# A state-space network on one core: the late plan with decays in SBUF, one slice summed on TensorE, and projections of two chunks at a time

## The chip, the cores and the metric

The program runs on one NeuronCore of a Trainium2 chip. The metric is the device time of one execution in microseconds; each kernel is given by the median of several runs. TensorE is called PE, VectorE DVE, ScalarE ACT, GpSimd POOL, and SyncE, which issues the transfers, SP.

## The reference

The network has two layers over a 64 x 64 image with 96 channels. Each layer is a mixer and then a small MLP on the 4096 tokens, both with a residual. The mixer of the second layer is what matters here. It normalizes, projects to 192 inner channels and a gate, convolves, and then scans the image in four directions, with 16 states for each channel:

```python
dA = jnp.exp(dt_t[..., None] * A)
h = dA * h + (dt_t * u_t)[..., None] * B_t[:, None, :]
y = jnp.sum(h * C_t[:, None, :], axis=-1)
...
yy = y[0] + wh_y + inv_y[0] + invwh_y
yy = yy * jax.nn.silu(z)
return yy @ W_out.T
```

The MLP normalizes each token over its 96 channels, rounds to an 8-bit float, multiplies to 384 hidden units, adds a bias, takes the relu, rounds again and multiplies back to 96:

```python
h = jax.nn.relu(_qlinear(x, W1, b1))
y = _qlinear(h, W2, b2)
```

## The kernel before

The scans of the second layer are tiled by six groups of 32 channels and four quarters of the 16 states. A tile has 128 partitions, 32 channels times 4 states, and 4096 positions in time, in four slices of 1024. So there are 24 passes, one for each group and quarter. A pass scans rows and columns, forward and backward: 16 scan instructions of 1024 elements on DVE (`scan`, line 2007). A scan needs two inputs. One is the decay, an exponential that ACT computes in `decay_into` (line 1992); it lies in `two`, two PSUM tiles of 1024 columns named `da`, which the scans use in turn. The other is the input product in SBUF, which POOL makes. After the scans of a slice POOL adds the two column scans into `hs` (`add_columns`, line 2012), PE adds the row scans to it with identity matrices (lines 2018 and 2022), ACT fetches the sum, POOL multiplies it by C (`times_c`, line 2035), and PE folds the four states of a channel into the accumulator `acc` (`sum_states`, line 2046). After four passes a group is complete.

For most of the passes the order of this work is written out by hand, by positions in the sequence of scans. The end is different. From the position `first_late` on, in the middle of the last pass, instructions are collected in an object of the class `Order`. Each has an engine, a price, what it reads, writes and takes from a pool of buffers, and an urgency `lead`, set for each chunk from the list `LATE`. `Order.run` then lists them on their engines by the prices. Only the order in which each engine is given its instructions comes out of this, and the waits follow from the data. An engine takes its instructions strictly in that order.

The late plan holds the last ten scans, the products of the last pass, the gate, the output projection, and the MLP of all tokens, in eight chunks of 512 tokens. Its steps, in the order of the data:

- The projection of channel group four for chunks 4 to 7 (`early`, lines 2312 and 2314): PE puts the residual chunk and the product of `ye`, the stored result of that group, into a bank, and ACT copies the sum back to `res` (line 2323). For other groups and chunks this has been done in the passes before.
- For slices `a` in `BY_SUMS`, PE adds the row scans and `hs` in a bank (line 2332), ACT fetches that (2346), and POOL multiplies by C (2348). For other slices POOL adds (2352) and multiplies (2353).
- The last row scans `x2s` are multiplied by C by DVE or POOL in halves of 512 (line 2358; POOL for the slices in `TIMES_POOL`). PE folds both products into `acc` (2282). Line 2285 adds the skip term.
- DVE multiplies `acc` by the gate (2363). PE projects, for each of the two chunks in a slice, with 32 rows and 96 columns at a time (`mixed`, 2371), and DVE adds the bank to `res` (2392).
- MLP (`late_chunk`): DVE takes statistics (2397), ACT and DVE make the inverse root (2400, 2401), DVE normalizes by token column in four pieces of 96 (2405), PE transposes (2411), ACT copies (2414), PE multiplies by the first weights (2418), ACT or DVE casts from PSUM (2420, `ROUND_DVE`), DVE or ACT adds the bias and takes the relu (2424 and 2422, `RELU_ACT`), POOL casts to 8 bits (2425), PE multiplies by the second weights (2430), ACT copies (2433), DVE or POOL adds the bias (2435, `BIAS_POOL`) and the residual (2437, `LAST_POOL`), and SP stores the chunk (2438).

The late plan keeps its buffers in free parts of `x0s` and `x1s`, and takes PSUM banks from `late` and, once the last scan has read its decay, from `da`.

Of the kernel before, what the change touches and what calls it, by code (L numbers as in the profile page):

```python
# [126 lines left out]
BY_SUMS, TIMES_POOL = (0, 1), (0, 3)  # L127
ROUND_DVE, RELU_ACT = [(2, 2), (5, 1), (5, 2), (6, 2), (7, 0)], [(0, 1), (2, 1), (5, 0), (7, 1)]
BIAS_POOL, LAST_POOL = (0, 1, 6), (0, 1, 2, 3)
LATE = (103.0, 38.0, -4.0, -6.0, -9.0, -12.0, -12.0, -13.0)  # L130
# [125 lines left out]
class Net:  # L256
# [1636 lines left out]
    def scans(self, xs, out):  # L1893
# [14 lines left out]
        with ExitStack() as ctx:  # L1908
# [208 lines left out]
            def load_y(f, m):  # L2117
                rows = (slice(0, P), slice(P, P + GC))[f]
                if f == 0 or m == 0:
                    self.ye = self.ye[::-1]  # L2120
                to = slice(GC * (m % 3), GC * (m % 3) + GC) if f else slice(0, P)
                inputs[f, m] = self.ye[0][to], self.tail_w[f][to]
                keep(nc.sync.dma_start(self.ye[0][to], self.y_d[rows, chunk(m)]))
# [15 lines left out]
            pairs += [(1, i, k) for i, k in ((n - 3, 2), (n - 2, 2), (n - 1, 3)) for k in range(k)]  # L2139
# [95 lines left out]
            for p in range(first_late + 1, len(seq)):  # L2235
                i, o, e = seq[p]
                das[p] = das[pos[i, o, e - 1]] if e == NS else 1 - das[p - 1]
# [22 lines left out]
            own, ident8, b2h = carve(P), carve(P, FP8, 1), carve(CD, F16, 2)  # L2260
            for tag, k, form in (
                ("st", 4, lambda: carve(12).rearrange("p (j s) -> p j s", s=3)),
                ("sd", 4, lambda: carve(4)),
                ("x8", 3, lambda: tokens(carve(4 * CD, FP8, 1))),
                ("xt", 3, lambda: carve(CH, BF16, 2)[0:CD]),
                ("h16", 6, lambda: carve(CH, F16, 2)),
                ("h8", 3, lambda: carve(nm * CH, FP8, 1).rearrange("p (m t) -> p m t", m=nm)),
                ("o16", 3, lambda: tokens(carve(4 * CD, F16, 2))),
            ):
                od.slots(tag, [form() for _ in range(k)])  # L2270
            od.slots("bank", [ph.tile([P, CH], F32, tag="hs", name=f"late{i}") for i in range(2)])
            od.slots("hc", [hcs[(NS * last + a) % 3] for a in range(2)])
# [4 lines left out]
            od.add("POOL", 0.3, lambda: keep(pool.tensor_copy(b2h, b2)), w=["b2h"])  # L2277

# [10 lines left out]
            od.add("SEQ", 0.0, lambda: od.free["hc"].append((0.0, hcs[(NS * last + 2) % 3])), r=["times", "sums"], w=["third"])  # L2289
# [9 lines left out]
            def open_banks():  # L2299
                od.free["bank"] += [(0.0, t[:, h * CH : (h + 1) * CH]) for t in two for h in range(nh)]  # L2300

            od.add("SEQ", 0.0, open_banks, r=[("S", 0, both - 1), ("da", 0), ("da", 1)], w=["open"])
# [5 lines left out]
            def early(m):  # L2308
                def f():
                    y, w = inputs.pop((1, m))  # L2310
                    o = tokens(at["eo", m][:, 0 : 4 * CD])
                    keep(nc.tensor.matmul(o, self.ident, self.res[:, m], start=True, stop=False))
                    for j in range(4):
                        keep(nc.tensor.matmul(o[:, j], y[:, j:CH:4], w, start=False, stop=j == 3))

                return f

            for m in range(4, NCH):
                if m == 7:
                    od.add("SP", 0.65, lambda: load_y(1, 7), w=[("ye", 1)], kb=64)  # L2320
                od.lead = LATE[m]
                od.add("PE", 1.6, early(m), r=[("ye", m % 3)], new={("eo", m): "bank"})
                od.add("ACT", 0.46, lambda m=m: keep(act.copy(self.res[:, m], tokens(at["eo", m][:, 0 : 4 * CD]))), r=[("eo", m)], w=[("res", m)])

# [3 lines left out]
            def presum(a, h):  # L2328
                def f():
                    s = chunk(turn[last % 2][1][a] * nh + h)  # L2330
                    for k, t in enumerate((h0, hs)):
                        keep(nc.tensor.matmul(at["s", a, h], self.ident, t[:, s], start=k == 0, stop=k == 1))  # L2332
# [3 lines left out]
            for a in range(NS):  # L2336
# [5 lines left out]
                A = ("A", a)  # L2342
                if a in BY_SUMS:
                    for h in range(nh):
                        od.add("PE", 1.8, presum(a, h), r=ready, new={("s", a, h): "bank", **({("hc", a): "hc"} if h == 0 else {})})
                        od.add("ACT", 0.6, lambda a=a, h=h: keep(act.copy(at["hc", a][:, half(h)], at["s", a, h])), r=[("s", a, h), ("hc", a)], w=[(A, h)])
                    for h in range(nh):
                        od.add("POOL", 1.27, lambda a=a, h=h, t=times: keep(pool.tensor_tensor(at["hc", a][:, half(h)], at["hc", a][:, half(h)], t[:, half(h)], ALU.mult)), r=[("hc", a)], w=[(A, h)])
                    od.add("PE", 0.95, lambda a=a, m0=m0: fold([at["hc", a][:, half(h)] for h in range(nh)], m0, False), r=[("hc", a), (A, 0), (A, 1)], w=[A])
                else:  # L2350
                    t = hs[:, part[j]]
                    od.add("POOL", 2.36, lambda t=t, j=j: keep(pool.tensor_tensor(t, t, h0[:, part[j]], ALU.add)), r=ready, w=[(A, 0)])
                    od.add("POOL", 2.36, lambda t=t, c=times: keep(pool.tensor_tensor(t, t, c, ALU.mult)), r=[(A, 0)], w=[(A, 0)])
                    od.add("PE", 0.95, lambda t=t, m0=m0: fold([t[:, half(h)] for h in range(nh)], m0, False), r=[(A, 0)], w=[A])
                xp = x[:, part[j]]
                for h in range(nh):
                    e, cost = ((nc.vector, 0.67), (nc.gpsimd, 1.27))[a in TIMES_POOL]
                    od.add(("DVE", "POOL")[a in TIMES_POOL], cost, lambda e=e, h=h, xp=xp, t=times: keep(e.tensor_tensor(xp[:, half(h)], xp[:, half(h)], t[:, half(h)], ALU.mult)), r=[("S", 0, NS + a)], w=[("xc", a, h)])
                od.add("PE", 0.95, lambda xp=xp, m0=m0: fold([xp[:, half(h)] for h in range(nh)], m0, True), r=[A, "sums", ("skip", m0 // NQ), ("xc", a, 0), ("xc", a, 1)], w=[("fx", a)])

                b, q = divmod(m0, NQ)
                r = slice(GC * q, GC * q + nh * GC)
                od.add("DVE", 0.72, lambda r=r, b=b: keep(dve.tensor_tensor(gu[r, b], acc[r, b], gz[r, b], ALU.mult)), r=[("fx", a)], w=[("y", a)])

                def mixed(m0=m0):
                    for j in range(4):
                        for m in range(m0, m0 + nh):
                            b, q = divmod(m, NQ)
                            r = slice(GC * q, GC * q + GC)
                            o = tokens(at["o", m][:, 0 : 4 * CD])  # L2370
                            keep(nc.tensor.matmul(o[:, j], gu[r, b, j:CH:4], self.tail_w[2][r], start=True, stop=True))

                od.add("PE", 1.1, mixed, r=[("y", a)], new={("o", m): "bank" for m in range(m0, m0 + nh)})
# [5 lines left out]
    def late_chunk(self, od, m, ov, ident8, b2h):  # L2379
# [7 lines left out]
        st, sd, x8, xt, h8, o16 = ((k, m) for k in ("st", "sd", "x8", "xt", "h8", "o16"))  # L2387
# [3 lines left out]

        od.add("DVE", 0.58, lambda: keep(dve.tensor_tensor(x, x, tokens(at["o", m]), ALU.add)), r=[("o", m)], w=[("res", m)])
# [6 lines left out]
        od.add("DVE", 0.56, stats, r=[("res", m)], new={st: "st"})  # L2399
        od.add("ACT", 0.3, lambda: keep(act.activation(at[sd], at[st][:, :, 2], AF.Sqrt, bias=self.eps5, scale=1.0 / CD)), r=[st], new={sd: "sd"}, table="sqrt")  # L2400
        od.add("DVE", 0.17, lambda: keep(dve.reciprocal(at[sd], at[sd])), w=[sd])

        def normed():
            for j in range(4):
                keep(dve.tensor_scalar(at[x8][:, j], x[:, j], at[st][:, j, 1:2], at[sd][:, j : j + 1], ALU.subtract, ALU.mult, saturate=False))

        od.add("DVE", 0.68, normed, r=[("res", m), st, sd], new={x8: "x8"})
# [5 lines left out]
        od.add("PE", 0.55, turned, r=[x8, "ident8"], new={("t", m): "bank"})  # L2413
        od.add("ACT", 0.6, lambda: keep(act.copy(at[xt], at["t", m][0:CD])), r=[("t", m)], new={xt: "xt"})
        for i in range(nm):
# [3 lines left out]
            e, f, cost = (("ACT", act.copy, 0.6), ("DVE", dve.tensor_copy, 0.65))[(m, i) in ROUND_DVE]  # L2419
            od.add(e, cost, lambda f=f, h=h, k=k: keep(f(at[k], at[h])), r=[h], new={k: "h16"})  # L2420
            if (m, i) in RELU_ACT:
                od.add("ACT", 0.65, lambda k=k, b=b: keep(act.activation(at[k], at[k], AF.Relu, bias=b)), w=[k])
            else:
                od.add("DVE", 0.42, lambda k=k, b=b: keep(dve.tensor_scalar(at[k], at[k], b, 0.0, ALU.add, ALU.max)), w=[k])
# [7 lines left out]
        od.add("PE", 1.0, down, r=[h8, *(("h8", m, i) for i in range(nm))], new={("f", m): "bank"})  # L2432
        od.add("ACT", 0.47, lambda: keep(act.copy(at[o16], tokens(at["f", m]))), r=[("f", m)], new={o16: "o16"})
        e, f, cost = (("DVE", dve, 0.3), ("POOL", pool, 0.8))[m in BIAS_POOL]
        od.add(e, cost, lambda f=f: keep(f.tensor_tensor(at[o16], at[o16], b2h.unsqueeze(1).to_broadcast([P, 4, CD]), ALU.add)), r=["b2h"], w=[o16])
        e, f, cost = (("DVE", dve, 0.58), ("POOL", pool, 0.9))[m in LAST_POOL]
        od.add(e, cost, lambda f=f: keep(f.tensor_tensor(x, x, at[o16], ALU.add)), r=[o16], w=[("res", m)])
        od.add("SP", 0.65, lambda: keep(nc.sync.dma_start(ov[:, m], x)), r=[("res", m)], kb=192)
# [126 lines left out]
```

## Time and profile before

| What | Value |
|---|---|
| Runs | 1263.56 us median of 3, 1262.83 to 1267.61 |
| Profiled execution | 1267.05 us, of which the span is 1265.2 us |
| PE, matmuls | 1042.1 us busy, 82% of the span |
| DVE | 1138.5 us busy, 90% |
| ACT | 884.0 us busy, 70% |
| POOL | 847.7 us busy, 67% |
| Start of the first late scan | 1177.74 us |
| Last store issued | 1262.2 us |

Busy time is the time in which an engine has an instruction of the program in work, also if that instruction stands and waits for something inside the engine. The span begins with the first instruction and ends with the last one; the rest of the execution's time lies around it. A group of instructions is shown with its line in the kernel, the engine, the operation, output and inputs by the program's names, shapes, count, busy time and mean duration in nanoseconds, and then the idle time of the engine just before these instructions with what ended it.

### The profile page before, as it was taken

To read this page: it belongs to the slowest core of one execution; us is meant where nothing else is said; L and a number is where in the kernel's file an instruction comes from. 1 tells how busy PE (TensorE), PEld (TensorE's weight loads), DVE (VectorE), ACT (ScalarE), POOL (GpSimd) and SP (SyncE) were. 2 spreads that over 40 slices of the span, in tenths; PEclk is the share of its full clock that TensorE was granted. 3 is DMA by queue.
4 is the path that set the end of the run, shared out by engine and by line. 5 is a ranking of instruction groups with operands and counts; after the bars stand their busy time and mean duration, and the time that the engine had idled before them with its cause. 6 is when DMAs were issued, how large, how long until landed. Compare 5 with 4: busy or idle time off the path is not lost.

```text
span 1265.2 us, 11505 instructions
## 1 busy us (share of the span) xinstructions
PE 1042.1 (82%) x3666; PEld 427.2 (34%) x3666; DVE 1138.5 (90%) x922; ACT 884.0 (70%) x1068; POOL 847.7 (67%) x517
## 2 busy tenths in 40 slices
PE   9998988987367788897778877787778889898886
PEld 7632233322122222332222222333223444333434
DVE  6395698577989999999999999999999999999787
ACT  4455566545677878888778877888778878777435
POOL 3000385243277878978888878988888878976566
PEclk9999989997578888888878889898789999888875
DMA  2062110146755665545735675545736766423201
GB/s 74 13 171 77 26 26 13 50 152 209 232 172 158 224 219 196 149 137 178 243 126 157 224 209 206 148 139 175 239 126 196 241 210 222 149 80 93 78 1 51
DMA packets 79134, 183.17 MB, mean 145 GB/s; under 512 B 21534, under 2 KB 34936, under 8 KB 77688
## 3 DMA queue, kind: packets, MB, share of 16 engines
q1 hardware_dynamic: 78376, 182.16, 45.7%
q8 instruction: 31, 0.51, 0.2%
q14 instruction: 39, 0.32, 0.1%
q10 hardware_dynamic: 688, 0.19, 0.1%
HBM read 159.73 MB, written 21.52 MB: 143 GB/s over the span
## 4 chain that ended last, share of the span: by engine, by line
DVE 41%; PE 15%; issue 9%; ACT 4%; DMA 2%; POOL 1%; SPq 0%; another core or an unknown queue 0%; POOLq 0%; DVEq 0%; ACTq 0%
DVE xws L2007 13%; DVE h1s L2007 12%; DVE h0s L2007 7%; PE hs L2018 6%; PE hs L2022 3%; DVE x1s L2007 3%; DVE x0s L2007 2%; DVE x2s L2007 2%; ACT da L1992 2%; ACT xws L1977 1%; DMA kept<-xn 1%; PE acc L2046 1%; POOL hss L2012 1%; DMA x2s<-bc 1%; PE late L2332 1%
## 5 line engine op out<-in xcount | busy, mean ns | idle before, releaser
L2035 POOL TENSOR_TENSOR kept<-kept,kept 128x1024 f32<-128x1024 f32 x92 | 216.9, 2358 | 81.9 <-issue 39.8
L2012 POOL TENSOR_TENSOR hss<-h1s,xws 128x1024 f32<-128x1024 f32 x96 | 228.1, 2378 | 60.0 <-DVE xws L2007 57.2
L2018 PE MATMUL hs<-h0s,ident 128*128 128x512 f32 x360 | 220.1, 697 | 28.0 <-DVE h0s L2007 24.1
L1992 ACT ACTIVATE da<-dt1s,a 128x1024 f32<-128x1024 f32 x168 | 187.5, 1117 | 69.3 <-DVE xws L2007 54.7
L2007 DVE TENSOR_TENSOR_SCAN xws<-da,xws 128x1024 f32<-128x1024 f32 x96 | 222.1, 2313 | 12.4 <-ACT da L1992 12.3
L1992 ACT ACTIVATE da<-dt0s,a 128x1024 f32<-128x1024 f32 x166 | 185.1, 1116 | 39.7 <-DVE h0s L2007 16.1
L2022 PE MATMUL hs<-hss,ident 128*128 128x512 f32 x368 | 189.1, 606 | 21.4 <-POOL hss L2012 21.4
L2007 DVE TENSOR_TENSOR_SCAN h1s<-da,h1s,xws 128x1024 f32<-128x1024 f32 x72 | 167.6, 2328 | 0.8 <-ACT da L1992 0.5
L2046 PE MATMUL acc<-kept,fold 128*32 128x512 f32 x368 | 88.7, 694 | 68.5 <-POOL kept L2035 68.5
L2031 ACT COPY kept<-hs 128x512 f32<-128x512 f32 x184 | 107.1, 582 | 48.5 <-PE hs L2022 47.7
L2018 PEld LDWEIGHTS hs<-h0s,ident 128*128 128x128 f32 x360 | 71.3, 215 | 152.8 <-issue 82.3
L2022 PEld LDWEIGHTS hs<-hss,ident 128*128 128x128 f32 x368 | 69.4, 193 | 120.6 <-issue 78.8
L2018 PE MATMUL hs<-x0s,ident 128*128 128x512 f32 x128 | 73.5, 658 | 13.8 <-DVE x0s L2007 13.8
L2018 PE MATMUL hs<-x1s,ident 128*128 128x512 f32 x128 | 72.4, 650 | 13.4 <-DVE x1s L2007 13.4
L1971 POOL TENSOR_TENSOR x1s<-x1s,dus 128x1024 f32<-128x1024 f32 x32 | 75.5, 2361 | 8.8 <-DMA x1s<-bc 8.8
L2018 PE MATMUL hs<-x2s,ident 128*128 128x512 f32 x120 | 67.5, 646 | 14.5 <-DVE x2s L2007 14.5
L1971 POOL TENSOR_TENSOR x2s<-x2s,dus 128x1024 f32<-128x1024 f32 x32 | 75.8, 2367 | 0.3 <-DMA x2s<-bc 0.3
L2007 DVE TENSOR_TENSOR_SCAN x0s<-da,x0s 128x1024 f32<-128x1024 f32 x32 | 74.0, 2313 | 1.1 <-ACT da L1992 1.1
L2007 DVE TENSOR_TENSOR_SCAN x1s<-da,x1s 128x1024 f32<-128x1024 f32 x32 | 74.0, 2313 | 1.1 <-ACT da L1992 1.1
L2007 DVE TENSOR_TENSOR_SCAN x2s<-da,x2s 128x1024 f32<-128x1024 f32 x32 | 74.1, 2316 | 0.9 <-ACT da L1992 0.7
L1244 POOL MEMSET pairs<- 96x256 f32 x1 | 0.3, 308 | 103.3 <-ACTq L309 103.3
L1977 ACT COPY xws<-x1s 128x1024 f32<-128x1024 f32 x32 | 63.4, 1980 | 5.2 <-POOL hss L2012 5.2
(372 smaller groups left out, 1973.7 us busy)
## 6 DMA issues: line engine op xcount, KB each, us to landing
kept<-bc SPq DMA_DIRECT2D x92, 512.0 KB
x2s<-bc SPq DMA_DIRECT2D x32, 512.0 KB
x0s<-bc SPq DMA_DIRECT2D x28, 512.0 KB
x1s<-bc SPq DMA_DIRECT2D x28, 512.0 KB
dus<-du SPq DMA_DIRECT2D x20, 512.0 KB
dt1s<-dt SPq DMA_DIRECT2D x20, 512.0 KB
dt0s<-dt SPq DMA_DIRECT2D x20, 512.0 KB
kept<-xn SPq DMA_DIRECT2D x24, 384.0 KB
```

The source lines that it names most:

```text
L1244: nc.gpsimd.memset(self.pairs1[:, :, 0 : HW + 2 : HW + 1, :], 0.0)
L1971: keep(nc.gpsimd.tensor_tensor(x, x, du[:, part[j]], ALU.mult))
L1977: keep(copy(grid(xw)[:, w, :], cols(xs[i % 3])[:, w, :]))
L1992: keep(nc.scalar.activation(t, dts[o][:, part[j]], AF.Exp, scale=self.a6[:, g, k : k + 1]))
L2007: keep(nc.vector.tensor_tensor_scan(to, da, x, start, ALU.mult, ALU.add))
L2012: keep(nc.gpsimd.tensor_tensor(cols(hs)[:, w, :], grid(h1)[:, w, :], grid(xw)[:, w, :], ALU.add))
L2018: keep(nc.tensor.matmul(t, self.ident, x[:, chunk(m)], start=k == 0, stop=False))
L2022: keep(nc.tensor.matmul(sums[i, m], self.ident, hs[:, chunk(m)], start=False, stop=True))
L2031: keep(nc.scalar.copy(to, sums.pop((i, j * (SC // CH) + h))))
L2035: keep(nc.gpsimd.tensor_tensor(t, t, times_c_by(i, a), ALU.mult))
L2046: keep(nc.tensor.matmul(to, self.fold4, src, start=k == 0, stop=k == NK - 1))
L2332: keep(nc.tensor.matmul(at["s", a, h], self.ident, t[:, s], start=k == 0, stop=k == 1))
```

## The change

The late plan is given new settings and new steps.

- Nine of the ten late scans read their decay from two new SBUF tiles, carved from `x0s`. The PSUM tiles `da` serve as banks as soon as the first late scan is done.
- Only slice 0 is summed on PE, now with the last row scans `x` too. DVE multiplies this sum by C from the bank, and ACT's fetch and POOL's product of it are gone. Slices 1 to 3 are added and multiplied on POOL. The products of the last row scans of slices 1 and 3 go to POOL, those of slice 2 to DVE.
- The projection works on two chunks at once. Two tiles `blocks` hold the weights of a group twice, on the diagonal of a 64-row block, so one matmul takes 64 rows in and gives 192 columns. For chunks 4 to 7 the product of group four opens the banks in which the product of the last group is then added. The residual is no longer put through PE, and DVE adds each bank to half of two chunks of `res`. The load of `ye` for chunk 7 is issued with those of chunks 4 to 6.
- The normalization is two operations of 384 elements with broadcast statistics on DVE (five chunks) or four pieces on ACT (three chunks).
- Relus, casts, bias and last adds are shared out anew: relus go to POOL in nine cases, to ACT in six and to DVE in nine; one bias add and no last add is left on POOL.
- Prices and urgencies are new.

```diff
-BY_SUMS, TIMES_POOL = (0, 1), (0, 3)
-ROUND_DVE, RELU_ACT = [(2, 2), (5, 1), (5, 2), (6, 2), (7, 0)], [(0, 1), (2, 1), (5, 0), (7, 1)]
-BIAS_POOL, LAST_POOL = (0, 1, 6), (0, 1, 2, 3)
-LATE = (103.0, 38.0, -4.0, -6.0, -9.0, -12.0, -12.0, -13.0)
+BY_SUMS, TIMES_POOL = (0,), (1, 3)
+ROUND_DVE = ((1, 1), (1, 2), (2, 0), (3, 0), (4, 2), (5, 1), (7, 0))
+RELU_ACT = ((1, 0), (3, 0), (3, 2), (5, 0), (6, 0), (7, 0))
+RELU_POOL = ((0, 0), (0, 1), (1, 1), (1, 2), (2, 0), (2, 1), (2, 2), (3, 1), (4, 0))
+NORM_ACT, BIAS_POOL, LAST_POOL = (1, 3, 4), (0,), ()
+LATE = (266.0, 520.0, 182.0, 420.0, -46.0, -128.0, -287.0, 1415.0)
...
-                das[p] = das[pos[i, o, e - 1]] if e == NS else 1 - das[p - 1]
+                das[p] = das[pos[i, o, e - 1]] if e == NS else 5 - das[p - 1] if p > first_late + 1 else 2
...
+            blocks = [carve(2 * CD) for _ in range(2)]
+            two += [carve(SC) for _ in range(2)]
...
-            od.add("SEQ", 0.0, open_banks, r=[("S", 0, both - 1), ("da", 0), ("da", 1)], w=["open"])
+            od.add("SEQ", 0.0, open_banks, r=[("S", 1, NS)], w=["open"])
...
+            def blocked(key, y, w, r, first, end):
                 def f():
+                    for k in range(2):
+                        o = at[key, k][:, 0 : 4 * CD].rearrange("p (j e) -> p j e", j=2)
+                        for j in range(2):
+                            keep(nc.tensor.matmul(o[:, j], y[r, 2 * k + j : CH : 4], w[r], start=first and j == 0, stop=end and j == 1))
...
+                        od.add("PE", 0.9, summed(a, h, h0, True, False), r=ready[-1:], new={key: "bank"})
+                        od.add("PE", 0.9, summed(a, h, hs, False, False), r=whole, w=[key])
+                        od.add("PE", 0.9, summed(a, h, x, False, True), r=[("S", 0, NS + a)], w=[key])
+                        od.add("DVE", 0.69, lambda h=h, xp=xp, t=times, key=key: keep(dve.tensor_tensor(xp[:, half(h)], at[key], t[:, half(h)], ALU.mult)), r=[key], w=[("xc", a, h)])
...
+        if m in NORM_ACT:
+            od.add("DVE", 0.18, rate, r=[sd], w=[st])
+            od.add("ACT", 1.2, normed, r=[*both, st, sd], new={x8: "x8"})
+        else:
+            od.add("DVE", 0.6, lambda: keep(dve.tensor_tensor(at[xc], x, spread(at[st][:, :, 1]), ALU.subtract)), r=[*both, st], new={xc: "xd"})
+            od.add("DVE", 0.57, lambda: keep(dve.tensor_tensor(at[x8], at[xc], spread(at[sd]), ALU.mult, saturate=False)), r=[xc, sd], new={x8: "x8"})
...
             if (m, i) in RELU_ACT:
-                od.add("ACT", 0.65, lambda k=k, b=b: keep(act.activation(at[k], at[k], AF.Relu, bias=b)), w=[k])
+                od.add("ACT", 0.74, lambda k=k, b=b: keep(act.activation(at[k], at[k], AF.Relu, bias=b)), w=[k])
             else:
-                od.add("DVE", 0.42, lambda k=k, b=b: keep(dve.tensor_scalar(at[k], at[k], b, 0.0, ALU.add, ALU.max)), w=[k])
+                e, f, cost = (("DVE", dve, 0.5), ("POOL", pool, 0.85))[(m, i) in RELU_POOL]
+                od.add(e, cost, lambda f=f, k=k, b=b: keep(f.tensor_scalar(at[k], at[k], b, 0.0, ALU.add, ALU.max)), w=[k])
```

## The prediction

> **What bounds the kernel now.** Up to the 1178th microsecond the two kernels issue the same instructions on DVE, ACT, POOL and PE; on SP only one 64 KB load has moved. So I read the tail alone, from 1177.74 us (start of the first scan that the late plan issues) to the last store. The view of busy time by stretches splits it where its limit changes:
>
> ```profile
> core 0: us, PE busy (x) PEld busy (x) DVE busy (x) ACT busy (x) POOL busy (x), PEclk, DMA share, GB/s
> 1177.70:1211.30 33.60, 29.63 (x84) 15.06 (x82) 24.67 (x12) 14.10 (x19) 21.18 (x13) 0.80 0.05 18
> 1211.30:1223.30 12.00, 8.30 (x60) 4.50 (x56) 11.38 (x14) 1.13 (x3) 12.00 (x7) 0.99 0.00 1
> 1223.30:1262.20 38.90, 32.00 (x192) 17.72 (x188) 33.08 (x92) 21.59 (x45) 22.08 (x32) 0.54 0.09 32
> ```
>
> Stage A is the last ten scans, B the products that POOL still owes afterwards (POOL busy 12.00 of 12.00), C the MLP of eight chunks (DVE 33.1 of 38.9, the fullest). In A DVE is idle for 8.9 us. The groups of the tail say why:
>
> ```profile
> L2007 DVE TENSOR_TENSOR_SCAN h0s<-da,h0s,x2s 128x1024 f32<-128x1024 f32 x3 | 7.0, 2334 | 5.1 <-ACT da L1992 5.1
> L2323 ACT COPY res<-late 128x384 f32<-128x384 f32 x4 | 1.9, 479 | 10.3 <-PE late L2314 10.3
> ```
>
> A scan waits for its decay, and the decay stands on ACT behind copies that wait for PE's early projections (in the chain of waits 0.84 + 2.03 us each). Next I asked the timeline what a scan and a POOL instruction do to each other, and what two DVE and POOL products do:
>
> ```profile
> 1182.96 2.33 DVE L2007 TENSOR_TENSOR_SCAN h0s<-da,h0s,x2s 128x1024 f32<-128x1024 f32 x1
> 1182.32 2.37 POOL L2012 TENSOR_TENSOR hss<-h1s,xws 128x1024 f32<-128x1024 f32 x1
> ...
> 1212.43 0.70 DVE L2358 TENSOR_TENSOR x2s<-x2s,dus 128x512 f32<-128x512 f32 x1
> 1212.55 2.80 POOL L2353 TENSOR_TENSOR hss<-hss,dus 128x1024 f32<-128x1024 f32 x1
> 1213.06 2.84 DVE L2358 TENSOR_TENSOR x2s<-x2s,dus 128x512 f32<-128x512 f32 x1
> ```
>
> The scan, whose decay lies in PSUM, runs over the POOL add and neither is longer for it. The product has both inputs in SBUF: alone 0.70, the next one 2.84 because it stands until POOL's instruction ends, and POOL's own 2.80 because it stood behind the first. The two take turns.
>
> **What the Trainium skill says.** "SBUF — State Buffer", Who interferes with whom: "A DVE instruction with two SBUF inputs contends with a GpSimd instruction that reads SBUF"; the one that comes second is blocked for the whole instruction. The lines above agree, for a tensor_tensor. No scan of this trace with both inputs in SBUF (two at L1841, 2.28 and 2.35 us) had a POOL instruction beside it, so for scans it is inferred. "VectorE: DVE Perf Modes", Mode 2×_2P: a tensor_scalar can spend both read ports on one tensor. The trace agrees: L2405 takes 0.32 alone and 1.18 beside POOL. "GPSIMD Engine Reference", 4.1 Engine selection: a one-input operation there is roughly line-rate; L2425 (one input, 128x512) takes 0.61 undisturbed.
>
> **The change, part by part.**
>
> *Decays in SBUF (A).* Nine of the ten late scans read a decay from SBUF, so by the rule above they alternate with every POOL instruction beside them. POOL's `times` ends at 1182.1 in both kernels. From there, in the order of the changed program, the pair carries nine scans at 2.37 (two in a row took 4.75), 21.3; four column adds at 2.37, 9.5; two casts, 0.56; and the first two adds of `h0` at 2.36, 4.7: 36.1 us, last scan at 1218.2 against 1211.26, **+7.0**. DVE first or POOL first does not matter, as all of it is due before B can end. The memsets (two, 0.3) read nothing and are left out. Gone is the wait for ACT, 8.8 us of 33.5: what comes late next is the pair. Bounds: +5 if small pieces slip between, +9 with a hop of 0.1 to 0.2 at each of 17 turns.
>
> *Early projections (A, C).* Gone are four times 2.9 us of PE and four ACT copies (0.48, and their 10.3 us of waiting). Their cover is the pair, so nothing more is gained. In come two block projections for chunks 4 to 7 and four later ones, each 8 matmul rows with 64 rows in and 192 columns out. No such row is shown here; between eight and sixteen of the present steps (16 in 2.1 us at L2371) I take 2.2 each. PE loses 11.6 us here and some 5 of row sums, and nothing waits for it in A: 0. The weight blocks cost ACT eight copies at about 0.3 (rows of 128x4 and 128x96 take 0.30 and 0.34). They wait for POOL's memsets, the second of which stands behind two column adds, to about 1191.9; queued behind them on ACT is the decay of a scan that the turns put at about 1196.6, so it has 4.7 us for four copies (1.2) and itself (1.12): 0, but 1 to 2 us if POOL fell back further. The adds into `res` stay 8 of 384 elements at 0.53. The load of chunk 7 (issued at 1182.92) moves on SP's queue to the three loads at 1146.7, past four loads of C and two of `u`; it waits for the same PE step as the third load did and delays the first C load, at 1150.09, by its own issue of about 0.3, and nothing reads that before 1202: 0.
>
> *Products (B).* Row sums by PE fall from two slices to one, whose product DVE takes from PSUM (2 x 0.61, under POOL: 0). Slice 1 falls to POOL as a whole. After the last scan POOL has four products or adds at 2.36 and four at 1.27, 14.5, with two DVE halves between them (1.2): 15.7 and a gap or two, 16.1 against 12.06: **+4.0** (bounds +2, +5).
>
> *MLP (C).* DVE: 11 fewer biased relus at 0.512, -5.6; normalization from 32 pieces (11.4) to ten broadcast operations at 0.70 (the same form at L1479 has means 0.689 and 0.714) and three small ones at 0.17, -3.9; two more casts from PSUM 1.4, two more bias adds 0.7, four more last adds at 0.635, 2.5: -4.9. ACT: +2 relus at 0.734, -2 casts at 0.589, +12 pieces of 96 at 0.34 (nearest row L577): +4.4. POOL: nine relus in, two bias adds (1.0) and four last adds (0.94) out. A relu of 128x512 on POOL is not shown: from below 0.61 (the cast), from above 1.5 (a straight line through POOL's TENSOR_SCALAR, 0.22 for one column and 0.46 for 96). I take 1.0: +3.2. DVE comes to 28 of the stage, POOL and ACT to 25 and 26. But the chunk's own chain gets longer where a relu at 0.35 becomes 1.0 in front of a POOL cast, and broadcasts and POOL still take turns. I take **-1** (bounds -4, +4.5).
>
> Sum: 7.0 + 4.0 - 1 = **+10 us**. The profiled run took 1267.05 (span 1265.2 and 1.85 around it), which would become 1277; it was 3.5 above the median of the runs, 1263.56, so the median goes to 1273.6, say **1274**. With the bounds, 1267 to 1282.
>
> **Rivals.** *The scans do not take turns with POOL* (the chip treats a scan unlike a tensor_tensor). Then nine scans run through from 1180.7, with two products: 1203.3, 8 earlier. POOL's column adds end at 1192.6, then 14.2 + 5.1 + 1.2 of products: 1213.1, 10 earlier. With C -1 the end comes 11 earlier, 1253. For it: scans are slow (2.3 ns an element) and might leave the port free. Against: the wording above, and L2358.
>
> *C gives it back.* Before, the fold of the last slice waits on PE behind first-layer matmuls: POOL is done at 1223.3, the last gate runs at 1231.3. In the new order it stands behind two transposes only. If these 8 us and the lighter DVE both count, C is 9 shorter and the end 2 later: 1266. Against: DVE had only 1.4 us idle there, other chunks filled the time.
>
> *POOL becomes the bound of C.* Relus at 1.5 put POOL at 30 us and in turn with every DVE operation: C +4.5, 1279.
>
> **How the numbers follow.** Forecast 0.55; POOL the bound of C 0.18; given back 0.12; no turns 0.15. A measurement of this kernel can tell about 0.5%, 6.3 us. Slower by more: 0.5 of the forecast, all of the POOL case, a little of the third: 0.70. Within: 0.15. Faster: the last case, 0.15. The range 1262 to 1284 takes in the first three and leaves out the last and a tail.
>
> **What would show it.** In the changed profile: scans of the tail at 3 to 4.7 us (waiting counts as busy) in turn with POOL adds that also stretch; last scan near 1218; POOL's last product near 1234; DVE no longer waiting for `da`. Tail scans at 2.35 beside POOL adds at 2.37, with the last one near 1203, would refute the forecast. The mean of the relus on POOL, near 0.6 or near 1.5, decides C.

## The result and the profile after

The changed kernel takes **1279.08 us** (median of 4 runs, 1276.69 to 1281.86), the kernel before 1263.19 beside it: 1.0127 times as long, with a 95% interval of 1.0081 to 1.0173, so 15.9 us more. The profiled execution took 1281.86 us, its span 1280.1. The first late scan starts at 1177.92, within 0.2 us of before. So the tail alone is longer, and its three stretches show where. The view is busy time by stretches, as before: A, the scans; B, POOL's owed products; C, the MLP.

```profile
core 0: us, PE busy (x) PEld busy (x) DVE busy (x) ACT busy (x) POOL busy (x), PEclk, DMA share, GB/s
1177.90:1217.00 39.10, 18.79 (x56) 7.60 (x54) 38.02 (x13) 13.28 (x19) 36.95 (x13) 0.73 0.04 14
1217.00:1230.40 13.40, 11.39 (x27) 5.21 (x29) 7.82 (x13) 0.60 (x2) 13.38 (x7) 0.50 0.00 1
1230.40:1277.10 46.70, 32.50 (x180) 19.17 (x177) 31.57 (x71) 26.38 (x57) 35.56 (x34) 0.54 0.08 28
```

Cut at the exact events (table below), stage A has grown by 5.6 us, B by 1.3 and C by 7.8. In A DVE now has something in work for 38.0 of 39.1 us and POOL for 37.0. That is not more work. The groups of DVE in stage A show what it is:

```profile
L2009 DVE TENSOR_TENSOR_SCAN x2s<-x0s,x2s 128x1024 f32<-128x1024 f32 x4 | 15.8, 3958 | 0.2
...
L2009 DVE TENSOR_TENSOR_SCAN h0s<-x0s,h0s,x2s 128x1024 f32<-128x1024 f32 x2 | 8.8, 4388 | 0.0
L2009 DVE TENSOR_TENSOR_SCAN h0s<-da,h0s,x2s 128x1024 f32<-128x1024 f32 x1 | 2.3, 2329 | 0.0
...
L2348 DVE TENSOR_TENSOR x2s<-da,dus 128x512 f32<-128x512 f32 x2 | 1.3, 666 | 0.0
```

A scan of one form takes 2.33 us with its decay in `da` (PSUM; this one is the last before the ten, its end lies in the window) and 4.39 with its decay in `x0s` (SBUF). The 5.1 us in which `h0s` waited for ACT are gone, and so are the ACT copies into `res`. What DVE does instead of waiting for ACT is to stand inside its own instruction. The timelines of DVE and of POOL (start, duration, engine, line) show for whom:

```profile
1195.47 4.38 DVE L2009 TENSOR_TENSOR_SCAN h0s<-x0s,h0s,x2s 128x1024 f32<-128x1024 f32 x1
1199.89 12.85 DVE L2009 TENSOR_TENSOR_SCAN x2s<-x0s,x2s 128x1024 f32<-128x1024 f32 x3
...
1193.36 8.65 POOL L2014 TENSOR_TENSOR hss<-h1s,xws 128x1024 f32<-128x1024 f32 x2
1202.09 8.50 POOL L2351 TENSOR_TENSOR hss<-hss,h0s 128x1024 f32<-128x1024 f32 x2
```

POOL's adds take 4.3 each (two in 8.65) where they took 2.37, and the scans 4.3 each (three in 12.85): each starts about 2.2 us after the other one and stands until that is through. The products of 512 out of PSUM (L2348, 0.67), which ran beside a POOL product, are not held up, where L2358 with both inputs in SBUF had been (2.84).

In stage C the groups of POOL are these:

```profile
L2439 POOL TENSOR_SCALAR x1s<-x1s,b 128x512 f16<-128x512 f16 x9 | 19.4, 2163 | 8.3 <-DVE x1s L2434 8.3
L2440 POOL CAST x1s<-x1s 128x512 fp8e5<-128x512 f16 x24 | 15.6, 689 | 0.0
```

A relu takes 2.16 us, and the idle column of the casts is 0.0. In the kernel before POOL was idle for 14.0 us in front of the same 24 casts:

```profile
L2425 POOL CAST x0s<-x0s 128x512 fp8e5<-128x512 f16 x24 | 15.6, 664 | 14.0 <-DVE x0s L2424 11.4 <-ACT x0s L2422 1.0 <-PE late L2411 0.9
```

From its first relu at 1238.7 to its last cast, which ends at 1274.3, POOL has no gap in the changed kernel. Who waits for it, in the view of waits of stage C (waiting instruction, releaser, us in total, times, longest):

```profile
PEld L2445 <- POOL x1s L2440: 13.6, 12, 3.6
...
PE da L2445 <- POOL x1s L2440: 8.2, 9, 3.4
...
DVE res L2452 <- POOL x1s L2450: 4.4, 1, 4.4
```

The second matmul of the MLP waits for POOL's casts, and DVE once, up to 1258.5, for POOL's one bias add, which stands behind relus and casts in POOL's list.

### The profile page after: what moved, and what is told of

Read it like the earlier page. It is cut to its first block, busy times and chain, and to the rows that moved or that the text cites. A ratio compares the mean times of both kernels' runs of the same rounds, so it can differ in the third digit from the quotient of the medians.

```text
span 1280.1 us, 11358 instructions
## 1 busy us (share of the span) xinstructions
PE 1039.3 (81%) x3602; PEld 423.3 (33%) x3602; DVE 1146.5 (90%) x900; ACT 887.5 (69%) x1080; POOL 878.3 (69%) x520
## 4 chain that ended last, share of the span: by engine, by line
DVE 40%; PE 12%; issue 9%; POOL 5%; ACT 4%; DMA 2%; another core or an unknown queue 0%; POOLq 0%; DVEq 0%; SPq 0%; ACTq 0%
DVE xws L2009 13%; DVE h1s L2009 12%; DVE h0s L2009 7%; PE hs L2020 6%; DVE x2s L2009 3%; PE hs L2024 3%; DVE x0s L2009 2%; DVE x1s L2009 2%; ACT da L1994 2%; ACT xws L1979 2%; POOL hss L2014 2%; DMA kept<-xn 1%; POOL x1s L2439 1%; DMA dt<-hss 1%; POOL x1s L2440 1%
## 5 line engine op out<-in xcount | busy, mean ns | idle before, releaser
L2014 POOL TENSOR_TENSOR hss<-h1s,xws 128x1024 f32<-128x1024 f32 x96 | 235.8, 2459 | 57.7 <-DVE xws L2009 54.8
L1994 ACT ACTIVATE da<-dt1s,a 128x1024 f32<-128x1024 f32 x165 | 184.2, 1117 | 69.8 <-DVE xws L2009 54.9
L2009 DVE TENSOR_TENSOR_SCAN xws<-da,xws 128x1024 f32<-128x1024 f32 x93 | 217.3, 2337 | 9.0 <-ACT da L1994 9.0
L1994 ACT ACTIVATE da<-dt0s,a 128x1024 f32<-128x1024 f32 x161 | 179.6, 1115 | 38.2 <-DVE h0s L2009 15.4
L2020 PE MATMUL hs<-x1s,ident 128*128 128x512 f32 x128 | 75.3, 673 | 12.5 <-DVE x1s L2009 12.5
L1973 POOL TENSOR_TENSOR x0s<-x0s,dus 128x1024 f32<-128x1024 f32 x28 | 66.3, 2369 | 0.0
```

The costliest lines, as they stand in the source:

```text
L1973: keep(nc.gpsimd.tensor_tensor(x, x, du[:, part[j]], ALU.mult))
L1994: keep(nc.scalar.activation(t, dts[o][:, part[j]], AF.Exp, scale=self.a6[:, g, k : k + 1]))
L2009: keep(nc.vector.tensor_tensor_scan(to, da, x, start, ALU.mult, ALU.add))
L2014: keep(nc.gpsimd.tensor_tensor(cols(hs)[:, w, :], grid(h1)[:, w, :], grid(xw)[:, w, :], ALU.add))
L2020: keep(nc.tensor.matmul(t, self.ident, x[:, chunk(m)], start=k == 0, stop=False))
```

## The experiments

The three stages of every kernel, cut at the same three events in its own trace (start of the first late scan, end of the last, end of POOL's last product, end of the last add), with the ratio of its runs to runs of before taken beside them:

| Kernel | A | B | C | A+B+C | Median, us | Ratio (95%) |
|---|---|---|---|---|---|---|
| before | 33.5 | 12.1 | 38.8 | 84.4 | 1262.8 to 1263.6 | 1 |
| after | 39.1 | 13.4 | 46.6 | 99.1 | 1279.1 | 1.0127 (1.0081 to 1.0173) |
| e1: after, decays in PSUM | 25.2 | 9.6 | 47.4 | 82.2 | 1261.4 | 0.9985 (0.9967 to 1.0003) |
| e2: after, no relu on POOL | 39.1 | 13.4 | 41.2 | 93.7 | 1277.0 | 1.0102 (1.0071 to 1.0133) |
| e3: both of these | 25.2 | 9.6 | 40.3 | 75.1 | 1257.2 | 0.9955 (0.9939 to 0.9970) |
| e4: before, decays in SBUF | 38.6 | 14.7 | 36.9 | 90.2 | 1273.8 | 1.0078 (1.0049 to 1.0107) |
| e5: before, relus on POOL | 33.4 | 11.7 | 41.9 | 87.0 | 1269.5 | 1.0043 (1.0026 to 1.0060) |
| e7: e3, normalization in pieces | 25.2 | 9.3 | 43.1 | 77.5 | 1260.2 | 0.9972 (0.9960 to 0.9983) |
| e8: before, no early projections | 25.4 | 12.1 | 37.5 | 74.9 | 1254.9 | 0.9944 (0.9926 to 0.9963) |
| e9: e3, two slices summed by PE | 25.2 | 3.4 | 48.7 | 77.2 | 1259.3 | 0.9964 (0.9953 to 0.9974) |
| e10: e3, adds on POOL | 25.2 | 9.7 | 41.1 | 75.9 | 1256.6 | 0.9943 (0.9922 to 0.9965) |
| e11: e3, three relus on POOL | 25.3 | 9.6 | 41.2 | 76.1 | 1257.9 | 0.9954 (0.9939 to 0.9970) |

Two cautions on the table. The tails start between 1171.9 and 1180.3 us, though the instructions ahead of them differ in one load only. The stages leave this out; the medians do not, and the runs of one kernel spread over up to 11 us. And the trace of before is of a long execution (1267.05): against before, tails come out 0.3 to 4.0 us lower than the ratios say. The surplus seems to lie in C: e4 and e8, whose MLP plan is that of before, have 36.9 and 37.5 there, not 38.8. Among the variants of the changed kernel the stages agree closely wherever the program is the same: A is 39.1 twice and 25.2 to 25.3 six times.

**e1, decays back in PSUM.**

```diff
-                das[p] = das[pos[i, o, e - 1]] if e == NS else 5 - das[p - 1] if p > first_late + 1 else 2
+                das[p] = das[pos[i, o, e - 1]] if e == NS else 1 - das[p - 1]
...
-            od.add("SEQ", 0.0, open_banks, r=[("S", 1, NS)], w=["open"])
+            od.add("SEQ", 0.0, open_banks, r=[("S", 0, both - 1), ("da", 0), ("da", 1)], w=["open"])
```

> The changed kernel with its nine late decays back in the two PSUM tiles (the bank list opens after the third last scan of chunk 0 again). Theory (scans with both inputs in SBUF take turns with POOL): late scans go back to about 2.3 us beside POOL adds of 2.36, the last scan ends 3 to 6 us earlier than in the changed kernel, whose last one ends at 1217.0; the time falls by 3 to 6 us, to 1273 to 1276. Rival 1 (the late scans are slow for another reason, or the turns are hidden behind POOL's own list): time within 2 us of 1279. Rival 2 (PSUM banks run short, since early projections wait for them): scans at 2.3 but ACT's decays late again, last scan near 1217 and no gain. Whatever the relus on POOL cost stays: stage C remains near 46 us.

Measured: 1261.4, so 17.7 us gone. That is the whole loss: the ratio, 0.9985, cannot be told from that of before. The theory held as to the scans, and its size was far off. The timelines of DVE and of POOL in its stage A, where x0s has become da:

```profile
1186.96 7.20 DVE L2009 TENSOR_TENSOR_SCAN x2s<-da,x2s 128x1024 f32<-128x1024 f32 x3
...
1187.21 4.64 POOL L2351 TENSOR_TENSOR hss<-hss,h0s 128x1024 f32<-128x1024 f32 x2
1191.81 2.35 POOL L2352 TENSOR_TENSOR hss<-hss,dus 128x1024 f32<-128x1024 f32 x1
```

Three scans in 7.20 us instead of 12.85, over two adds in 4.64 instead of 8.50: for the scans one operand's place is all that differs. The edit also opens the banks of `da` later; e4, where they open as in the kernel before, shows the turns without that. The second rival, that banks run short, fell with A at 25.2. The expectation had set the turns against the *old* stage A, 33.5 us, in which DVE also waited for ACT. The new plan without turns does A in 25.2 and B in 9.6. So the turns cost the changed kernel 13.9 us in A and 3.8 in B, 17.7 together; C is 0.8 longer than in the changed kernel.

**e2, no relu on POOL.**

```diff
-RELU_POOL = ((0, 0), (0, 1), (1, 1), (1, 2), (2, 0), (2, 1), (2, 2), (3, 1), (4, 0))
+RELU_POOL = ()
```

> The changed kernel with the nine biased relus of POOL back on DVE, nothing else. Theory (POOL's relus at 2.16 us made POOL the bound of the MLP): POOL loses 19.4 us of the last stage, DVE gains 9 x 0.5 = 4.5 us; the stage shrinks from 46.6 to 38 or 39 us, the time falls by 7 to 9 us to 1270 to 1272, last scan unchanged at 1217. Rival (the stage is long because of the broadcast normalization or of the chunk's own chain): the time falls by less than 3 us, or rises because DVE carries 4.5 us more.

Measured: 1277.0; A and B stay, C falls from 46.6 to 41.2. The direction is the theory's, the size is not: the tail gains 5.4 us, and the medians differ by 2.1, which is inside the noise (the two intervals overlap). It was expected that C would return to the 38 or 39 of before, and it does not, so the rival has a part in it too: something besides the relus keeps C long. That the relus do cost time is clear from e3 against e1.

**e3, both edits.**

> The changed kernel with both of these edits: decays in PSUM and no relu on POOL. What is left of the change is one slice of row sums instead of two, the block projection and the broadcast normalization. Theory (the two causes add up): 1279 less 3 to 6 less 7 to 9, so 1264 to 1269, at or slightly above the kernel before (1263). Second theory (the rest of the change is worth its predicted 5 us of DVE in the last stage): 1256 to 1262, faster than before. Third (the two causes are one wait seen twice): about 1271, no better than the relus alone.

Measured: 1257.2, faster than before by 0.45% (0.30 to 0.61). The time is that of the second theory, and the two causes are separate, stage by stage (A and B those of e1, C near that of e2). The reason that the theory gave did not hold: what is left of the change gains 5.7 us by the ratio, but in A and B; the last stage, where it was expected, is not shorter than before. Against e1, which has the relus still on POOL, C is 7.1 us shorter and the ratio 0.0030 lower. Its stretches:

```profile
1175.40:1200.60 25.20, 17.37 (x44) 5.34 (x42) 24.14 (x13) 13.08 (x19) 22.97 (x15) 0.80 0.06 21
1200.60:1210.20 9.60, 9.60 (x35) 7.44 (x35) 9.36 (x18) 0.61 (x3) 9.60 (x5) 0.69 0.01 2
1210.20:1250.60 40.40, 29.12 (x184) 16.56 (x182) 31.06 (x75) 25.96 (x57) 16.66 (x26) 0.71 0.10 35
```

In A DVE is busy for 24.1 of 25.2 us and now with work: thirteen instructions as in the changed kernel, where they took 38.0. In C POOL is down to 16.7 us.

**e4, the decays in SBUF alone, in the kernel before.** The same edit of `das` as the change makes, two SBUF tiles for it, and the bank list waits for their scans.

```diff
+            two += [carve(SC) for _ in range(2)]
...
-            od.add("SEQ", 0.0, open_banks, r=[("S", 0, both - 1), ("da", 0), ("da", 1)], w=["open"])
+            od.add("SEQ", 0.0, open_banks, r=[("S", 0, both - 1), ("da", 2), ("da", 3)], w=["open"])
```

> The kernel before with one part alone: its nine late decays go to two SBUF tiles, all else as before. Theory (turns): nine scans of 4.2 to 4.4 us where POOL adds stand beside them, last scan 4 to 7 us later than the 1211.3 of before, POOL's product list shifted by as much; the time rises by 4 to 7 us to 1267 to 1270. Rival (the scans run over POOL's adds and the wait for ACT goes): nine scans of 2.3, last scan 5 to 8 us earlier, the time 3 to 8 us below before.

Measured: ratio 1.0078, or 9.8 us slower (by the traces A +5.1, B +2.6, C -1.9). The turns alone make the kernel slower in the old plan too, and less than in the new one, since part of them falls into DVE's old wait for ACT.

**e5, the relus on POOL alone, in the kernel before.** The new list and the choice of engine at line 2424; two of its nine relus are ACT's there, so seven move.

> The kernel before with one part alone: its nine biased relus of the new list on POOL, all else as before. Prices from the runs so far: 2.0 us alone on POOL, where two operations per element cost it 2.0 and one 1.5. Theory (the relus' 18 to 20 us of POOL lengthen the last stage whatever the rest of the plan is): POOL's 22 us there become 40 of about 44, the last stage grows by 4 to 7 us, the time to 1267 to 1270. Rival (the stage of before has POOL idle for 14 us, which hides them): within 2 us of before.

Measured: +5.4 us by the ratio (3.3 to 7.6); C 38.8 to 41.9, POOL in it from 22.1 to 34.7 us busy. The theory held as to the time, though it reckoned with nine relus; the stage grew by 3.1, less than its 4 to 7 (against the long execution of before). The 14 us in which POOL was idle do not hide the relus.

**e6, what makes the relu dear on POOL.** From e1, three relus of each form; six of the nine leave out the bias, and there is one execution. What counts is the length of the instructions:

```diff
+                form = RELU_POOL.index((m, i)) % 3 if (m, i) in RELU_POOL else 0
+                args = ((b, 0.0, ALU.add, ALU.max), (0.0, 0.0, ALU.add, ALU.max), (0.0, None, ALU.max))[form]
```

> The kernel of the decays in PSUM, its nine relus on POOL in three forms of three: bias pointer added and maximum with 0; 0.0 added and maximum with 0 (no pointer; the bias is left out); one operation only, maximum with 0 (the bias is left out). Six biases are left out of the result. Theory A (two operations cost POOL twice): the first two forms 2.0 us, the third near 1.0. Theory B (the pointer costs): the first 2.0, the other two near 1.0 or 0.61 like the cast. Theory C (any tensor_scalar on POOL is slow): all three near 2.0.

The timeline of POOL, with one instruction of each form (the first has one operation, the second the bias, the third, at 1236.83, two constants) and the casts behind them:

```profile
1221.19 1.49 POOL L2441 TENSOR_SCALAR x1s<-x1s 128x512 f16<-128x512 f16 x1 [8.55 <-DVE x1s L2434]
1222.67 2.00 POOL L2441 TENSOR_SCALAR x1s<-x1s,b 128x512 f16<-128x512 f16 x1
1224.63 1.73 POOL L2442 CAST x1s<-x1s 128x512 fp8e5<-128x512 f16 x3
...
1236.83 2.00 POOL L2441 TENSOR_SCALAR x1s<-x1s 128x512 f16<-128x512 f16 x1
```

All three of one operation took 1.49; the shortest with two operations took 2.00, with the pointer (the bias) and without. None of the three theories is right as it stood: a second operation costs 0.5, the pointer nothing, and one operation is already more than twice a cast (0.61).

**e7, the normalization as before.** From e3, the four tensor_scalar pieces on DVE for all eight chunks, nothing of it on ACT:

```diff
+        def pieces():
+            for j in range(4):
+                keep(dve.tensor_scalar(at[x8][:, j], x[:, j], at[st][:, j, 1:2], at[sd][:, j : j + 1], ALU.subtract, ALU.mult, saturate=False))
```

> The kernel with both edits (decays in PSUM, no relu on POOL; 1257.2), with the normalization of all eight chunks as before the change: four tensor_scalar pieces of 96 on DVE for each, none on ACT. The broadcast form and ACT's share were priced at 3.9 us of DVE gained. Theory 1 (DVE is the fullest engine of the last stage, so its load counts): slower by 2 to 4 us, 1259 to 1261. Theory 2 (the chunk's own chain sets the stage, broadcasts take turns with POOL anyhow): within 1.5 us of 1257. Theory 3 (pieces fit better): faster by over 1.5.

Measured: tail 77.5 against 75.1, ratio 0.9972 against 0.9955; DVE in C busy for 34.7 us against 31.1. This points to theory 1, by 2.4 us in the tail, but it is not shown: the two intervals of the ratios overlap.

**e8, before without its early projections.** Left out are the four early projections of group four with their copies (the `early` of lines 2312 to 2323), so chunks 4 to 7 lack that term.

```diff
-                od.add("PE", 1.6, early(m), r=[("ye", m % 3)], new={("eo", m): "bank"})
-                od.add("ACT", 0.46, lambda m=m: keep(act.copy(self.res[:, m], tokens(at["eo", m][:, 0 : 4 * CD]))), r=[("eo", m)], w=[("res", m)])
```

> The kernel before with its four early projections of chunks 4 to 7 left out altogether, the PE steps and the ACT copies into the results (these chunks lack that term). Its decays stay in PSUM. Theory (the ten us in which ACT waited for these projections held the decays, and this is what the changed plan's early projections without ACT copies take away): scans of stage A run without waiting for decays, the stage falls from 33.5 to 25 to 27 us, the time by 5 to 9 us. Rival (the stage is held by PE or by POOL's adds instead): the stage stays above 31 us, the time falls by less than 3.

Measured: A falls from 33.5 to 25.4, the time by 7.1 us by the ratio. That is the A of e3, to 0.2 us. So the gain of the new plan in A is what becomes possible when no ACT copy of a projection stands ahead of a decay. The run takes PE's part away with the copy, so it does not say which of the two matters.

**e9, two slices by PE's sums.**

```diff
-BY_SUMS, TIMES_POOL = (0,), (1, 3)
+BY_SUMS, TIMES_POOL = (0, 1), (1, 3)
```

> The kernel with both edits (1257.2), in which the row sums of slices 0 and 1 both go through PE, products out of PSUM on DVE, instead of slice 0 alone. POOL loses an add and a product of 1024 (4.7 to 5.2 us) ahead of the MLP, DVE takes two more products of 0.61, PE three more rounds of about 0.9 for each half. Theory (POOL's owed list sets stage B): stage B shrinks by 3 to 5 us and the time by 2 to 5, to 1252 to 1255. Rival (PE or the banks take POOL's place, since stage B has PE busy 9.6 of 9.6 us): within 1.5 us of 1257, or slower.

Measured: B falls from 9.6 to 3.4, as POOL's list is shorter, and C grows by 8.4. The rival held: nothing is gained (0.9964 against 0.9955). The timeline of PE around the end of the last scan (1203.2):

```profile
1200.80 1.98 PE L2322 MATMUL late<-h0s,ident 128*128 128x512 f32 x4
1202.62 1.88 PE L2322 MATMUL late<-hss,ident 128*128 128x512 f32 x4
1204.34 1.88 PE L2322 MATMUL late<-x2s,ident 128*128 128x512 f32 x4
1206.15 1.06 PE L2292 MATMUL acc<-x2s,fold 128*32 128x512 f32 x8
```

The row sums hold PE for 5.4 us and the folds come after them: as far as this trace shows, PE took the place of POOL.

**e10 and e11, towards a better version.** e10 puts the bias and last adds of before back on POOL, e11 three of the nine relus.

```diff
-NORM_ACT, BIAS_POOL, LAST_POOL = (1, 3, 4), (0,), ()
+NORM_ACT, BIAS_POOL, LAST_POOL = (1, 3, 4), (0, 1, 6), (0, 1, 2, 3)
```

> The kernel with both edits (decays in PSUM, no relu on POOL), with the bias and last adds of before on POOL again: two more bias adds and four last adds, at about 0.94 us each on POOL for 0.45 and 0.6 on DVE. POOL is idle for some 23 of 40 us in the last stage, DVE for 9. Theory (DVE's load counts in the last stage): DVE loses 3.3 us, the time falls by 1 to 3 us to 1254 to 1256. Rival (the chunk's chain counts, and the adds on POOL are 0.3 to 0.5 longer at its end): within 1 us, or up to 2 slower.

```diff
-RELU_POOL = ()
+RELU_POOL = ((1, 1), (2, 1), (4, 0))
```

> The kernel with both edits, but three of the nine relus (second of chunk 1 and of chunk 2, first of chunk 4) on POOL. POOL then carries 16.7 + 3 x 2.0 of some 40 us. Theory (POOL hurts only where it is the bound; with three relus it is not): within 1 us of the kernel with both edits. Rival (each relu on POOL stands in front of its own chunk's cast, 2.0 instead of 0.35, and this lag itself costs): 1 to 2 us slower in proportion, three ninths of the 4 to 7 us that nine cost.

Neither can be told from e3 (0.9943 and 0.9954 against 0.9955). DVE's busy time in C did not fall in e10 (31.0 in e3, 31.1 in e10), so e10 does not test whether DVE's load counts. Three relus on POOL cost nothing that these runs can tell: POOL is then busy for 23.7 of 41.2 us. The rival's 1 to 2 us lie within the noise and stay open. Against e1, which differs from e11 in six relus alone, C is 6.2 us shorter and the ratio 0.9954 for 0.9985. e3, e10 and e11 are all faster than both kernels.

## Why the prediction was right, and where its steps were not

Forecast were +10 us and 1274, with slower at 0.70; measured were +15.9 and 1279.1, inside the range. The sign came from the right step. The sum is better than its terms: the MLP was missed beyond its own bounds (-4 to +4.5), and that the time stayed in the range was in part luck.

- **Decays in SBUF, +7.0: right.** +5.6 by the trace. A scan with both inputs in SBUF takes turns with POOL, which was inferred from a tensor_tensor and is now shown for the scan by e1 and e4, which undo and make this one step. What was off is the price of a turn. The sum used 2.37 us, the whole length of an instruction alone; a scan and an add together take 4.3 to 4.4, or about 2.2 for one. Against 2.33 + 2.37 = 4.70 for the two apart, an estimated 0.2 us of each instruction lies outside what they exclude each other from.
- **What comes next when ACT's wait goes: right.** "What comes late next is the pair." The rival without turns had the last scan at 1203.3, which is 25.6 us behind the first one; with the decays in PSUM the stage takes 25.2. The rival was refuted for this kernel, but its stage was priced well.
- **Products, +4.0: too much.** +1.3. By the shorter turns POOL had one 1024 product more done ahead of the last scan's end: 13.4 us of list were left, not 16.1. e9 shows besides that POOL's list is no full measure of the path: 6.2 us less of it came back as 8.4 us of stage C.
- **MLP, -1: wrong, +7.8.** The failing term is a relu on POOL. It was taken at 1.0 and bounded at 1.5 by a straight line through narrower instructions; it is 2.0 undisturbed and 2.16 on average. Nine times 1.16 is 10.4 us more on POOL, which came to 35.6 us instead of the 25 of the sum. Without these relus C is 5.4 us shorter (e2), so they are the larger part of the miss, and not all of it. DVE came to 31.6, not 28: its relus took 0.65 on average, its last adds 0.70 and its bias adds 0.51, where 0.51, 0.64 and 0.35 had been taken. So the rival **"POOL becomes the bound of C"** (0.18) took place beside the forecast. Its 1279 equals the measured time by luck: it had +11 for A and B, where +6.9 came, and +4.5 for C, where +7.8 came. A smaller term is ACT's normalization, 0.34 for a piece by the nearest row and 0.46 in the trace; the twelve kept ACT busy for 4.6 us, not 4.1.
- **"C gives it back" (0.12): did not happen.** The last gate was to run sooner behind POOL's last product. It ran 9.9 us behind it (1240.3 against 1230.4), where it had run 8.0 behind.
- **C without those relus: not a gain either.** In e2 and e3 C is 41.2 and 40.3, longer than the 38.8 of before, though DVE is lighter in e3 (31.1 against 33.1). The lighter normalization may count, by about 2.4 us in the tail (e7, not clear of noise). In A and B together e3 is 10.8 us ahead of before, and C gives 1.5 of that back, or about 3 by the C of e4 and e8. What sets C then, with no engine above 80%, was not isolated. The granted TensorE clock in C differed from trace to trace, from 0.54 (before and changed) to 0.84 (e9), and its part is open too. It does not order the stage, as e9 has the longest C, and it is no rival to the relus: e1 and e11 both had 0.64, with 47.4 and 41.2 us.
- **The share of the causes.** By the medians: the decays cost 17.7 us in the changed kernel (19.8 without POOL's relus), the relus 2.1, which is within the noise (4.3 with the decays in PSUM, which is not), and the rest of the change gains 5.7 by the ratio. The prediction had set the turns against the old stage; they also cost what the new early projections had won, which e8 puts at 8.1 us of stage A.

The reading of "SBUF — State Buffer", Who interferes with whom, in the Trainium skill is confirmed and now covers the scan. "GPSIMD Engine Reference", 4.1 Engine selection, calls a one-input operation there roughly line-rate. The cast of 128x512 took 0.61 us undisturbed here, but the relu of the same size 2.0, and 1.49 with one operation: one price for one-input operations does not hold on POOL in these traces.

## What to carry to other kernels

Ask of every operand that is moved from PSUM to SBUF which engine shares SBUF with its reader: here 17.7 us followed from the place of nine operands, though each scan alone is no longer than before, and the busy share (DVE 38.0 of 39.1) looked like work. Set a new wait against the changed plan without it, not against the old stage, which has its own waits; only then is seen what else the change had gained. And do not extrapolate an instruction's price over size and form where it decides which engine is the bound: nine relus on POOL cost 4.3 us (e1 against e3), and three nothing that could be told from noise.

## What the runs showed of the hardware

- A scan with both inputs in SBUF and a POOL tensor_tensor exclude each other nearly throughout: in steady turns each takes 4.2 to 4.4 us, for 2.33 and 2.37 apart; with the decay in PSUM both keep their own length (e1). Small POOL work was held up too: the cast of 128x128 took 2.09 us behind a scan, 0.29 in e1. A memset of 128x192, which reads nothing, was not (0.25 to 0.27 us in both).
- On POOL a tensor_scalar of 128x512 in f16 takes 1.49 us with one operation and 2.00 with two, the same with a pointer for the scalar as with constants (e6), and the cast of the same size to fp8 takes 0.61 undisturbed.
- On DVE the operations of the normalization with a broadcast input (128x384) take 0.53 to 0.56 us where they ran free, and up to 1.50 in turn with POOL. Their means in the changed kernel are 0.74 and 0.58; estimated had been 0.70.
